# An expert's up products in 512 columns, and its transposes in one run

## The chip, the core and the metric

The kernel runs on one NeuronCore of a Trainium2 chip. The metric is the device time of one execution in microseconds, as the median of several runs. A core has five engines with a queue each: TensorE (PE in the profile, its weight loads PEld), VectorE (DVE), ScalarE (ACT), GpSimd (POOL) and SyncE (SP). Every queue is worked in its own order, and engines wait for each other by semaphores.

## The reference

The input is 4 x 2048 tokens of 512 numbers. Each token is normalised to `xn`, and the output is the input plus two branches:

```python
xn = layernorm(x)
# branch 1: random features, then a product with the features of the weights
feats   = c * exp(xn @ (xis * proj).T - 0.5 * |xn|^2 * xis^2)
attn    = feats @ weights.T                  # weights: the same features of input_weights
# branch 2: 64 experts, of which each token takes 8; CAP = 256 slots for an expert
g = einsum('ech,ehi->eci', dispatch, gate_w) # H = 512 in, I = 256 hidden
u = einsum('ech,ehi->eci', dispatch, up_w)
expert_out = einsum('eci,eih->ech', silu(g) * u, down_w)
# weighted back to the tokens, plus one shared expert for every token
out = x + attn + moe + shared(xn)
```

Everything is in float32.

## The kernel before

A float32 operand is cut into two parts in TensorE's `float32r` format: `upper` casts it on ACT, and `rest` subtracts the cast from the original on DVE. A product is then made in three passes over the same PSUM tile: upper x upper, upper x rest, rest x upper. `products` (line 103) issues these passes over the chunks of the contraction.

The execution has three stages. In the first, from the start to about 427 us, tokens are normalised, routed and transposed in blocks of 512, and every second block is finished in `dense`. The second stage is a loop over the 64 experts (lines 931 to 959). The last one works off the blocks that were left (`ends`). Between the experts, `late_attention` (line 571) works off attention products of these blocks: `ps_fu` makes features, `ps_y` multiplies them, and both lie in the PSUM pool `ps_sm` with its two buffers.

One turn of the expert loop does this for expert i:

- It asks for weights of later experts (SP's queue) and calls `hidden(i)` (line 792): for gate and up each, and for each of two halves of the hidden width, 12 products of 256 columns (4 chunks x 3 passes). The stationary operand is a 128 x 128 piece of a weight part, and the 256 columns are a part of the expert's tokens. That makes 48 products `ps_gu`. Then `gated` makes silu(g) * u from a tanh on ACT and two operations on DVE, and `upper` and `rest` cut the result into `ehT`.
- POOL's queue gets the gather for expert i + 4.
- `turn_slots(i + 1)` (line 762) transposes the tokens of the next expert, in 8 TensorE transposes `ps_t`, and cuts them into `gT`. The first one of the first expert alone is put behind an earlier product.
- `split_gates(i + 1)` cuts the next gate and up weights: two casts `gu_h` of 128 x 1024 on ACT and two subtractions `gu_l` on DVE.
- `down(i - 1)` (line 810) makes 12 products `ps_e` of 512 columns. After each six of them ACT scales the result by the token weights into `ye` (line 823), and POOL adds it to the output by an indirect DMA. Then `split_down(i)` cuts the down weights into `d_h` and `d_l`.

The program text does not give the queues' order: a scheduler in the compiler places each engine's instructions. It keeps dependencies, and the orders that `behind(a, b)` asks for. So transposes and attention products land between the expert's products where the scheduler puts them. [...] SBUF tiles of 4 KiB a partition come from the pool `four` with 40 slots.

Of the kernel before, what the change touches and what calls it, by code (L numbers as in the profile page):

```python
# [9 lines left out]
FP = mybir.dt.float32  # L10
# [3 lines left out]
ALU = mybir.AluOpType  # L14
# [4 lines left out]
P = 128  # L19
# [3 lines left out]
E = 64  # L23
# [5 lines left out]
CAP = 256  # L29
# [5 lines left out]
KC = H // P  # L35
RC = R // P
IC = I // P
# [16 lines left out]
def rfs_attention_moe_kernel(  # L54
# [15 lines left out]
    nc = tc.nc  # L70
# [5 lines left out]
    ps_mm = ctx.enter_context(tc.tile_pool(name="ps_mm", bufs=4, space=PSUM))  # L76
# [5 lines left out]
    act = ctx.enter_context(tc.tile_pool(name="act", bufs=4))  # L82

    def kib4(shape, name, dt=FPR):
        return four.tile(shape, dt, tag="four", name=name)
# [11 lines left out]
    def upper(dst, src):  # L97
        return nc.scalar.copy(dst, src)  # L98

    def rest(dst, src, hi, on=nc.vector):  # L100
        return on.tensor_tensor(dst, src, hi.bitcast(FP), ALU.subtract)  # L101

    def products(ps, w, v, start, stop):

        n = len(w)
        for part, (a, b) in enumerate(((0, 0), (0, 1), (1, 0))):
            for c in range(n):
                last["pe"] = nc.tensor.matmul(  # L108
                    ps,
                    w[c][a],  # L110
                    v[c][b],
                    start=(start and part == 0 and c == 0),
                    stop=(stop and part == 2 and c == n - 1),
                )
        return last["pe"]

    def behind(a, b):

        tc.add_manual_dep(a.ins, b.ins.name, ORDER, reason="what a needs comes late")
# [18 lines left out]
    def parts(pair, n, cols=slice(None)):  # L138
        hi, lo = pair
        return [(hi[c][:, cols], lo[c][:, cols]) for c in range(n)]  # L140
# [24 lines left out]
    last = {}  # L165
# [98 lines left out]
    def across(n):  # L264

        q = rt.tile([P, TB], FP, tag="q", name="q", bufs=3)
        nc.sync.dma_start(q, norms[n].partition_broadcast(P))
        return q
# [228 lines left out]
    def gated(dst, g, u):  # L497

        nc.scalar.activation(dst, g, AF.Tanh, scale=0.5)
        nc.vector.scalar_tensor_tensor(dst, dst, 1.0, g, ALU.add, ALU.mult)  # L500
        nc.vector.scalar_tensor_tensor(dst, dst, 0.5, u, ALU.mult, ALU.mult)  # L501

    def feature(fT, v, nsq, rc, ps):
        f = act.tile([P, TB], FP, tag="t", name="f")
        projected(v, rc, ps)
        exponent(f, nsq, rc, ps)
        nc.scalar.activation(f, f, AF.Exp, scale=ab[:, rc : rc + 1])  # L507
        upper(fT[0][rc], f)
        last["dve"] = rest(fT[1][rc], f, fT[0][rc])

    def attended(po, fT, s, start):

        return products(po, parts(fT, RC, ts(s, P)), parts(fW, RC), start, True)
# [55 lines left out]
    def fetch_block(b):  # L569

        xT = Chunks(KC, "xT_h"), Chunks(KC, "xT_l")
        for n, part in enumerate(xT):
            for k, t in enumerate(part.t):
                nc.sync.dma_start(t.bitcast(FP), turned[b // 2, n, :, 2 * k : 2 * k + 2, :])
        return xT

    def late_attention(blocks):

        blocks = list(blocks)
        nxt = fetch_block(blocks[0]), across(blocks[0])  # L580
        yield
        for n, b in enumerate(blocks):
            xu, nsq = nxt
            fT = Chunks(RC, "fU"), Chunks(RC, "fU")
            for rc in range(RC):
                ps = ps_sm.tile([P, TB], FP, tag="sm", name="ps_fu")
                feature(fT, parts(xu, KC), nsq, rc, ps)
                yield
            if n + 1 < len(blocks):
                nxt = fetch_block(blocks[n + 1]), across(blocks[n + 1])  # L590
            for s in range(NS):
                if s % 2 == 0:
                    yb = kib4([P, 2, H], "yb", FP)
                po = ps_sm.tile([P, H], FP, tag="sm", name="ps_y")
                attended(po, fT, s, True)
                last["dve"] = nc.vector.tensor_copy(yb[:, s % 2, :], po)
                if "down" in last:
                    behind(last["dve"], last["down"])
                if s % 2:
                    r0 = (b // 2) * TB + (s // 2) * UT  # L600
                    nc.sync.dma_start(
                        attn[r0 : r0 + UT, :].rearrange("(s p) d -> p s d", p=P), yb
                    )
                yield
# [20 lines left out]
    wn = across(NB)  # L625
# [28 lines left out]
    for rc in range(RC):  # L654
        pool, tag = ((ps_sm, "sm"), (ps_tr, "tr"))[rc // 2]
# [83 lines left out]
    def load_gates(e):  # L739
        gu = [kib4([P, KC, I], "gu", FP) for _ in range(2)]  # L740
        for t, w in zip(gu, (gw, uw)):
            nc.sync.dma_start(t, w[e].rearrange("(c p) i -> p c i", p=P))
        return gu

    def load_down(e):
        d = kib4([P, IC, H], "d", FP)
        nc.sync.dma_start(d, dw[e].rearrange("(c p) h -> p c h", p=P))
        return d

    def gather(e):  # L750
        xgs[e] = rows.tile([P, NH, XW], FP, tag="xw", name="xg")
        for h in range(NH):
            in_turn(
                nc.gpsimd.indirect_dma_start(  # L754
                    out=xgs[e][:, h, :],
                    out_offset=None,
                    in_=xnw,
                    in_offset=bass.IndirectOffsetOnAxis(ap=who[:, e, h : h + 1], axis=0),
                )
            )  # L760

    def turn_slots(e):
        xg = xgs.pop(e)
        xr = xg.bitcast(FPR)
        gp = [kib4([P, KC, CAP], "gT") for _ in range(2)]
        for c2 in range(KC // 2):
            pr = ps_tr.tile([P, 2, CAP], FPR, tag="tr", name="ps_t")
            ps = pr.bitcast(FP)
            for c in range(2):
                for h in range(NH):  # L770
                    turned_s = nc.tensor.transpose(  # L771
                        pr[:, c, ts(h, P)], xr[:, h, ts(c2 * 2 + c, P)], ident_r
                    )
                    if e == 0:
                        behind(turned_s, last["pe"])
            cs = slice(2 * c2, 2 * c2 + 2)
            upper(gp[0][:, cs, :], ps)
            turned_r = rest(gp[1][:, cs, :], ps, gp[0][:, cs, :])

        we = rt.tile([P, NH], FP, tag="we", name="we", bufs=4)  # L780
        shares = nc.vector.scalar_tensor_tensor(
            we, xg[:, :, H + e], 1.0, xg[:, :, H + E], ALU.add, ALU.mult
        )
        behind(shares, turned_r)
        nc.vector.reciprocal(we, we)
        wes[e] = we
        if e == 0:

            last["dve"] = shares
        return gp  # L790

    def hidden(e, gp, w):
        hi, lo = w
        v = [(gp[0][:, c, :], gp[1][:, c, :]) for c in range(KC)]
        gu = []
        for n in range(2):
            ps = ps_mm.tile([P, IC, CAP], FP, tag="mm", name="ps_gu")
            for ic in range(IC):
                wn = [(hi[n][:, c, ts(ic, P)], lo[n][:, c, ts(ic, P)]) for c in range(KC)]
                products(ps[:, ic, :], wn, v, True, True)  # L800
            gu.append(ps)
        g, u = gu
        sg = act.tile([P, IC, CAP], FP, tag="t", name="sg")
        gated(sg, g, u)
        hp = kib4([P, 2, IC, CAP], "ehT")
        upper(hp[:, 0], sg)
        last["dve"] = rest(hp[:, 1], sg, hp[:, 0])
        return hp
# [27 lines left out]
    xgs, wes, gps, gates, downs, gws, dws, hps = ({} for _ in range(8))  # L836
# [94 lines left out]
    for i in range(E + 1):  # L931


        if i + 2 < E:
            gates[i + 2] = load_gates(i + 2)
        if i + 1 < E:
            downs[i + 1] = load_down(i + 1)
        if i < E:
            hps[i] = hidden(i, gps.pop(i), gws.pop(i))
        next(slots, None)  # L940
        if i + 4 < E:
            gather(i + 4)
        if i + 1 < E:
            gps[i + 1] = turn_slots(i + 1)
            gws[i + 1] = split_gates(gates.pop(i + 1))
        for _ in range(rest_steps * i // E, rest_steps * (i + 1) // E):
            next(rest_of, None)
        if i >= E - 2:
            next(last_of)
        if i == E:  # L950

            next(last_of)
        if i > 0:
            down(i - 1, hps.pop(i - 1), dws.pop(i - 1))
        if i < E:
            dws[i] = split_down(downs.pop(i))
            if i == E - 2:

                last["down"] = last["split"]
# [40 lines left out]
```

## Time and profile before

| what | value |
|---|---|
| median of 3 runs | 1310.99 us (1310.63 to 1311.27) |
| the profiled execution | 1310.94 us, with a span of 1309.2 us |
| PE busy in the span | 1296.7 us, 99% |
| DVE busy | 925.0 us, 71% |
| ACT busy | 645.2 us, 49% |
| POOL busy | 581.7 us, 44% |
| products and transposes on PE | 7648 |

The span runs from the first instruction to the last. The 1.7 us between it and the execution's time lie outside of it. Matmuls are pipelined, so the end of a product in the profile is modelled: the pace of PE is read from the starts of rows, not from their lengths. ACT and DVE rows that follow without a wait overlap too, so what one costs its queue is also read from start to start.

### The profile page before, as it was taken

The numbers are of one execution on the slowest core, as the hardware profiler recorded it, in microseconds if no ns is written. First come the engines' busy times: TensorE is split into PE (matmuls) and PEld (weight loads), VectorE is DVE, ScalarE is ACT, GpSimd is POOL, SyncE is SP. The second block draws the span as 40 slices with busy tenths as digits, with TensorE's granted clock in tenths as the row PEclk, the third lists the DMA queues.
The fourth block names the chain that finished last, engine by engine and source line by source line (L and its number), as shares of the span: only waits on it lengthen the run. The fifth ranks groups of instructions, "written<-read, shape, count | busy, mean of one in ns | idle before, by whom it ended". The sixth has DMA issues, their size and how long they took to land.

```text
span 1309.2 us, 21368 instructions
## 1 busy us (share of the span) xinstructions
PE 1296.7 (99%) x7648; PEld 1138.6 (87%) x7648; DVE 925.0 (71%) x1922; ACT 645.2 (49%) x1017; POOL 581.7 (44%) x692
## 2 busy tenths in 40 slices
PE   8999999999999999999999999999999999999998
PEld 6888888888888999999999999999999999988886
DVE  7978768867865776777767677776776676643555
ACT  5643544354432555656566556555665566540111
POOL 3122022123106767877666667767676654210000
PEclk9999999999999999999999999999999999999999
DMA  7665675675586989999999999999999999784995
GB/s 255 242 213 205 244 279 199 238 286 212 201 307 193 317 226 330 259 290 272 304 282 266 292 272 274 246 321 262 282 256 303 280 261 233 206 239 168 318 319 193
DMA packets 189498, 338.61 MB, mean 259 GB/s; under 512 B 15952, under 2 KB 87632, under 8 KB 189392
## 3 DMA queue, kind: packets, MB, share of 16 engines
q1 hardware_dynamic: 153456, 245.93, 54.6%
q0 software_dynamic: 35936, 91.32, 29.7%
q8 instruction: 60, 0.98, 0.3%
q14 instruction: 46, 0.38, 0.1%
HBM read 220.66 MB, written 104.99 MB: 249 GB/s over the span
## 4 chain that ended last, share of the span: by engine, by line
PE 91%; DVE 4%; DMA 2%; SPq 1%; ACT 1%; issue 1%; POOL 0%; DVEq 0%; ACTq 0%
PE ps_gu L108 41%; PE ps_e L108 13%; PE ps_o L108 13%; PE ps_y L108 6%; PE ps_fu L108 6%; PE ps_f L108 4%; PE ps_t L771 3%; PE ps_x L331 2%; PE ps_l L364 2%; DMA xb<-in_L_attn_x_dram 1%; DVE st L275 1%; DMA xT_l<-turned 1%; SPq L262 1%; DVE xT_l L101 1%; DMA gu<-in_L_ffn_up_w_dram 0%
## 5 line engine op out<-in xcount | busy, mean ns | idle before, releaser
L824 POOL DMA_INDIRECT out_dram<-ye,who x128 | 225.3, 1760 | 189.3 <-ACT ye L823 140.9
L108 PE MATMUL ps_gu<-gT,gu_h 128*128 128x256 f32 x2048 | 290.0, 283 | 0.0
L108 PEld LDWEIGHTS ps_gu<-gT,gu_h 128*128 128x128 f32 x2048 | 267.2, 191 | 5.6 <-ACT gu_h L98 1.0
L701 POOL DMA_INDIRECT at<-upto,line x128 | 138.0, 1078 | 76.0 <-DVE first_of L695 37.3
L108 PE MATMUL ps_gu<-gT,gu_l 128*128 128x256 f32 x1024 | 167.0, 285 | 0.0
L101 DVE TENSOR_TENSOR gu_l<-gu,gu_h 128x1024 fp32r<-128x1024 f32 x128 | 155.7, 1218 | 6.9 <-ACT gu_h L98 6.9
L754 POOL DMA_INDIRECT xg<-xnw,who x128 | 137.3, 1073 | 39.0 <-issue 32.0
L108 PE MATMUL ps_e<-d_h,ehT 128*128 128x512 f32 x512 | 148.5, 391 | 0.0
L108 PEld LDWEIGHTS ps_gu<-gT,gu_l 128*128 128x128 f32 x1024 | 140.7, 191 | 0.3
L98 ACT CAST gu_h<-gu 128x1024 fp32r<-128x1024 f32 x128 | 132.4, 1058 | 0.0
L98 ACT CAST ehT<-sg 128x512 fp32r<-128x512 f32 x64 | 39.7, 621 | 156.3 <-DVE sg L501 156.3
L823 ACT ACTIVATE ye<-ps_e,we 128x512 f32<-128x512 f32 x128 | 88.6, 694 | 57.0 <-PE ps_e L108 56.1
L108 PEld LDWEIGHTS ps_e<-d_h,ehT 128*128 128x128 f32 x512 | 94.7, 188 | 18.8
L246 POOL TENSOR_TENSOR a<-rstd,ve 128x4 f32<-128x4 f32 x45 | 10.5, 233 | 200.1 <-DVE rstd L242 197.6
L501 DVE SCALAR_TENSOR_TENSOR sg<-sg,ps_gu 128x512 f32<-128x512 f32 x64 | 43.9, 686 | 68.4 <-PE ps_gu L108 68.0
L507 ACT ACTIVATE f<-f,ab 128x512 f32<-128x512 f32 x64 | 46.3, 723 | 82.0 <-DVE f L493 81.3
L101 DVE TENSOR_TENSOR d_l<-d,d_h 128x1024 fp32r<-128x1024 f32 x64 | 78.2, 1222 | 7.8 <-ACT d_h L98 7.4
L101 DVE TENSOR_TENSOR gT<-ps_t,gT 128x512 fp32r<-128x512 f32 x128 | 83.2, 682 | 0.2 <-ACT gT L98 0.2
L101 DVE TENSOR_TENSOR ehT<-sg,ehT 128x512 fp32r<-128x512 f32 x64 | 44.3, 692 | 51.5 <-ACT ehT L98 51.5
L108 PE MATMUL ps_o<-fW_h,fT 128*128 128x512 f32 x288 | 80.0, 392 | 0.2 <-ACT fT L98 0.2
L108 PE MATMUL ps_e<-d_l,ehT 128*128 128x512 f32 x256 | 79.3, 391 | 0.0
L108 PE MATMUL ps_o<-d_h,hT 128*128 128x512 f32 x256 | 79.1, 396 | 0.0
(181 smaller groups left out, 2526.8 us busy)
## 6 DMA issues: line engine op xcount, KB each, us to landing
gu<-in_L_ffn_gate_w_dram SPq DMA_DIRECT2D x64, 512.0 KB
gu<-in_L_ffn_up_w_dram SPq DMA_DIRECT2D x64, 512.0 KB
d<-in_L_ffn_down_w_dram SPq DMA_DIRECT2D x64, 512.0 KB
xnw<-xw SPq DMA_DIRECT2D x32, 577.0 KB
xb<-in_L_attn_x_dram SPq DMA_DIRECT2D x32, 512.0 KB
out_dram<-xb SPq DMA_DIRECT2D x32, 512.0 KB
xT_h<-turned SPq DMA_DIRECT2D x30, 512.0 KB
xT_l<-turned SPq DMA_DIRECT2D x30, 512.0 KB
```

Source lines behind the costliest of these rows:

```text
L98: return nc.scalar.copy(dst, src)
L101: return on.tensor_tensor(dst, src, hi.bitcast(FP), ALU.subtract)
L108: last["pe"] = nc.tensor.matmul(ps, w[c][a], v[c][b], start=(start and part == 0 and c == 0), stop=(stop and part == 2 and c == n - 1),)
L331: last["turn"] = nc.tensor.transpose(pr[:, ts(s, P)], src(s)[:, ts(kc, P)], ident if dt is FP else ident_r)
L364: logits = nc.tensor.matmul(pl, rwp[:, kc].rearrange("p t e -> p (t e)"), v[kc], start=(n == 0 and kc == 0), stop=(n == 1 and kc == KC - 1),)
L501: nc.vector.scalar_tensor_tensor(dst, dst, 0.5, u, ALU.mult, ALU.mult)
L507: nc.scalar.activation(f, f, AF.Exp, scale=ab[:, rc : rc + 1])
L701: nc.gpsimd.indirect_dma_start(out=at[:, e % TE, h, :], out_offset=None, in_=upto, in_offset=bass.IndirectOffsetOnAxis(ap=line[:, e, h : h ...
L754: nc.gpsimd.indirect_dma_start(out=xgs[e][:, h, :], out_offset=None, in_=xnw, in_offset=bass.IndirectOffsetOnAxis(ap=who[:, e, h : h + 1], ...
L771: turned_s = nc.tensor.transpose(pr[:, c, ts(h, P)], xr[:, h, ts(c2 * 2 + c, P)], ident_r)
L823: nc.scalar.activation(ye[:, h, :], po, AF.Copy, scale=wes[e][:, h : h + 1])
L824: now = nc.gpsimd.indirect_dma_start(out=out, out_offset=bass.IndirectOffsetOnAxis(ap=who[:, e, h : h + 1], axis=0), in_=ye[:, h, :], in_o ...
```

## The change

There are four edits.

1. In `hidden`, the gate is made as before. For up, the two token parts of a chunk lie side by side, so an upper weight part meets both of them in one product of 512 columns, and a rest weight part meets the upper token part in one of 256 columns. The left half of the PSUM tile collects two of the three passes and the right half the third. An ACT copy of the right half and a DVE addition of the left half (128 x 256 each) make `u` in SBUF. There are two such tiles for an expert, one for each half of the hidden width.
2. `turn_slots` lays `gT` out by pairs of chunks with both token parts together.
3. `turn_slots(e + 1)` is called inside `hidden(e)`, between gate and up. The first transpose of every expert is put behind the last gate product, and the next product behind the last transpose (`last["run"]`), so the eight stand together.
4. The attention results `yb` are copied from PSUM by ACT, not by DVE, and the order that kept the last ones behind a weight split is gone.

```diff
                     stop=(stop and part == 2 and c == n - 1),
                 )
+                if "run" in last:
+                    behind(last["pe"], last.pop("run"))
         return last["pe"]
...
                 attended(po, fT, s, True)
-                last["dve"] = nc.vector.tensor_copy(yb[:, s % 2, :], po)
-                if "down" in last:
-                    behind(last["dve"], last["down"])
+                nc.scalar.copy(yb[:, s % 2, :], po)
...
-        gp = [kib4([P, KC, CAP], "gT") for _ in range(2)]
+        gp = [kib4([P, 2, 2, CAP], "gT") for _ in range(KC // 2)]
...
-                    if e == 0:
+                    if c2 == c == h == 0:
                         behind(turned_s, last["pe"])
-            cs = slice(2 * c2, 2 * c2 + 2)
-            upper(gp[0][:, cs, :], ps)
-            turned_r = rest(gp[1][:, cs, :], ps, gp[0][:, cs, :])
+            upper(gp[c2][:, :, 0, :], ps)
+            turned_r = rest(gp[c2][:, :, 1, :], ps, gp[c2][:, :, 0, :])
+        last["run"] = turned_s
...
         hi, lo = w
-        v = [(gp[0][:, c, :], gp[1][:, c, :]) for c in range(KC)]
-        gu = []
-        for n in range(2):
-            ps = ps_mm.tile([P, IC, CAP], FP, tag="mm", name="ps_gu")
-            for ic in range(IC):
-                wn = [(hi[n][:, c, ts(ic, P)], lo[n][:, c, ts(ic, P)]) for c in range(KC)]
-                products(ps[:, ic, :], wn, v, True, True)
-            gu.append(ps)
-        g, u = gu
+        v = [gp[c // 2][:, c % 2] for c in range(KC)]
+        g = ps_mm.tile([P, IC, CAP], FP, tag="mm", name="ps_gu")
+        for ic in range(IC):
+            wn = [(hi[0][:, c, ts(ic, P)], lo[0][:, c, ts(ic, P)]) for c in range(KC)]
+            products(g[:, ic, :], wn, [(x[:, 0], x[:, 1]) for x in v], True, True)
+        if e + 1 < E:
+            gps[e + 1] = turn_slots(e + 1)
+        u = act.tile([P, IC, CAP], FP, tag="t", name="u")
+        for ic in range(IC):
+            ps = ps_mm.tile([P, 2, CAP], FP, tag="mm", name="ps_u2")
+            for c in range(KC):
+                for x, y in ((hi, slice(0, 2)), (lo, 0)):
+                    last["pe"] = nc.tensor.matmul(
+                        ps[:, y],
+                        x[1][:, c, ts(ic, P)],
+                        v[c][:, y],
+                        start=c == 0 and x is hi,
+                        stop=c == KC - 1 and x is lo,
+                    )
+                    if "run" in last:
+                        behind(last["pe"], last.pop("run"))
+            nc.scalar.copy(u[:, ic, :], ps[:, 1])
+            nc.vector.tensor_tensor(u[:, ic, :], ps[:, 0], u[:, ic, :], ALU.add)
         sg = act.tile([P, IC, CAP], FP, tag="t", name="sg")
         gated(sg, g, u)
...
         if i + 1 < E:
-            gps[i + 1] = turn_slots(i + 1)
             gws[i + 1] = split_gates(gates.pop(i + 1))
```

## The prediction

> **What bounds the kernel now.** I read the page first: who is full, whether TensorE runs at its full clock, and what the chain that ended last is made of.
>
> ```profile
> PE 1296.7 (99%) x7648; PEld 1138.6 (87%) x7648; DVE 925.0 (71%) x1922; ACT 645.2 (49%) x1017; POOL 581.7 (44%) x692
> PEclk9999999999999999999999999999999999999999
> PE 91%; DVE 4%; DMA 2%; SPq 1%; ACT 1%; issue 1%; POOL 0%; DVEq 0%; ACTq 0%
> ```
>
> PE is full, at full clock, and carries 91% of the chain. The sums by stage say the same of the expert stage: from 430 to 1143 us PE is busy 713.0 of 713 us, DVE 515.0, ACT 423.6, at a granted clock of 1.00. A busy PE need not be at its peak, so the next view is its timeline in a middle expert (columns: start, length, engine, line, what, count).
>
> ```profile
> 629.22 1.12 PE L108 MATMUL ps_gu<-gT,gu_h 128*128 128x256 f32 x8
> 630.18 0.64 PE L108 MATMUL ps_gu<-gT,gu_l 128*128 128x256 f32 x4
> 630.66 1.12 PE L108 MATMUL ps_gu<-gT,gu_h 128*128 128x256 f32 x8
> ...
> 632.10 0.80 PE L771 MATMUL ps_t<-ident_r,xg 128*128 128x128 f32 x8
> 632.74 1.16 PE L108 MATMUL ps_y<-fW_h,fU 128*128 128x512 f32 x4
> 633.74 1.08 PE L108 MATMUL ps_y<-fW_l,fU 128*128 128x512 f32 x4
> ...
> 636.47 1.07 PE L108 MATMUL ps_e<-d_h,ehT 128*128 128x512 f32 x4
> ...
> 638.28 1.12 PE L108 MATMUL ps_gu<-gT,gu_h 128*128 128x256 f32 x8
> ```
>
> Read from start to start: 12 products of 256 columns take 630.66 - 629.22 = 1.44 us, 0.120 each. From 633.74 to 638.28 there are 20 products of 512 columns: 4.54 us, 0.227 each. The eight transposes cost 0.64 us, and the four products behind them 1.00 instead of 0.91, so a run of eight costs 0.73. An expert's turn is 48 x 0.120 + 0.73 + 12 x 0.227 (down) + about 12 x 0.227 of attention = 11.9 us, just what the trace shows (626.35 to 638.28). There is no gap to win back, and none to spare: any late operand of PE is paid in full.
>
> Note the order at the end: attention, then down, then at once the next gate. Is the gate's weight there? ACT's timeline tells:
>
> ```profile
> 633.16 0.62 ACT L98 CAST ehT<-sg 128x512 fp32r<-128x512 f32 x1 [2.21 <-DVE sg L501]
> 633.68 1.07 ACT L98 CAST gT<-ps_t 128x512 fp32r<-128x512 f32 x2
> 634.64 1.06 ACT L98 CAST gu_h<-gu 128x1024 fp32r<-128x1024 f32 x1
> 637.12 0.69 ACT L823 ACTIVATE ye<-ps_e,we 128x512 f32<-128x512 f32 x1 [1.42 <-PE ps_e L108]
> 637.71 1.04 ACT L98 CAST gu_h<-gu 128x1024 fp32r<-128x1024 f32 x1
> 638.65 0.68 ACT L823 ACTIVATE ye<-ps_e,we 128x512 f32<-128x512 f32 x1
> ```
>
> The gate's cast `gu_h` ended at 635.70, 2.58 us before PE asked for it, because it stands ahead of both scalings `ye`. ACT's prices from these starts: `ehT` 0.52, `ye` 0.59, a cast 1.06 to its end. The sixth down product starts at 636.47 + 0.23 = 636.70 and has issued by 636.92; `ye` starts at 637.12, so PE hands over 0.20 later. From ACT to DVE or PE it is 0.03 (rows that waited). The prices of the rest are in the groups by form:
>
> ```profile
> L101 DVE TENSOR_TENSOR gu_l<-gu,gu_h 128x1024 fp32r<-128x1024 f32 x128 | 155.7, 1218 | 6.9 <-ACT gu_h L98 6.9
> L389 DVE TENSOR_TENSOR lt<-ps_lt,lt 128x256 f32<-128x256 f32 x16 | 6.7, 418 | 0.2
> L388 ACT COPY lt<-ps_lt 128x256 f32<-128x256 f32 x16 | 5.9, 368 | 12.6 <-PE ps_lt L381 10.4 <-DMA xnw<-xw 2.1
> ```
>
> **The change part by part.** *Wide products.* Per expert 24 up products of 256 become 8 of 512 and 8 of 256: 2.88 us become 8 x (0.227 + 0.120) = 2.78, -0.104; for 64 experts -6.7 us. The Trainium skill, TensorE: Matmul & The Clock Gate, section Back-to-back issue gap, gives N/2.4 + 2.5 ns, that is 109 and 216 ns. By that a merged product saves 2.5 ns and the kernel 512 x 2.5 = 1.3 us. The trace has 13 ns more than the columns need at both widths (120 - 107, 227 - 213), which gives the 6.7; I take the trace.
>
> *Transposes in one run.* Before, they stand in pieces for about half of the experts; a split of 4 + 4 costs 0.74 to 0.78 against 0.73, a split into shorter ones up to 0.1 more. -2 us (0 to -3).
>
> *DVE and ACT work.* 128 additions at 0.418 come to DVE (+53.5 us) and 28 `yb` copies at 0.686 go (-19.2): 515 + 34 of 713, no bound. ACT gets 128 copies at 0.368 and 28 at about 0.59: 424 + 64 of 713, no bound. Between up and silu's last step they add 0.2 + 0.37 + 0.42 = 1 us, hidden by the turn that lies between `hidden(i)` and `down(i)`. As busy time this is free. As places in a queue it is not.
>
> *The order of the queues.* In the built programs POOL's order is unchanged. SP has the same transfers, shifted a few places among each other; their data are asked for two experts ahead. PE and ACT are rearranged. A frequent turn:
>
> ```
>         PE                                          ACT, before the gate of the next expert
> before  gate+up 48, T 8, attention 12, down 12,     ehT, gT, gT, gu_h(gate), ye, gu_h(up), ye
> after   gate 24, T 8, up 16, down 12, attention n,  ... u, ye, ye, ehT, gu_h(gate), gu_h(up)
> ```
>
> Down now comes first and attention after it, and the scalings stand ahead of the gate's cast. ACT works in order, so the cast waits for the end of down. Counted from down's last issue to the first gate product: 0.20 hand-over + 0.59 second `ye` + 0.52 `ehT` + 1.06 cast + 0.03 = 2.40 us. PE covers it with n attention products of 0.227. Where an exponential (0.62) stands between, that is added. Then `gu_l`: it ends 0.03 + 1.22 after the cast, 8 gate products take 0.96, so another 0.29 unless two attention products stand there. The 63 turns, counted in the built order:
>
> - Both `ye` ahead of the cast, n = 0 to 2: 13 turns. Nine with n = 0 at 2.40, one with n = 2 at 1.95, three with n = 2 and an exponential at 2.57: 31.3, and 13 x 0.29 = 3.8.
> - n = 4 or 5: 6 turns, 4 x 1.50 + 2 x 1.89 = 9.8, and 1.7.
> - n = 7: 4 turns at 0.82 = 3.3, and 1.2.
> - n of 10 and more: 20 turns, most covered: 1.6 and 1.2.
> - The cast ahead of at least one `ye`: 20 turns, one of them late because `gT` stands there: 1.9 and 0.3.
>
> Sum 47.9 + 8.2 = +56 us. Beside it stand turns where another row in ACT's or DVE's queue (`u`, `fU`, `gT`) holds a cast or its subtraction: 0 to 63 x 0.29 = 18 us, +6 taken, as most have a gap to catch up in. `yb` copies now queue in ACT, and `ps_sm` has two buffers: 28 copies, each up to one cast (1.06) late, of which PE mostly finds other work; 0 to 10, +2 taken. At the end of the stage the last experts have no attention left to stand before their down: 0 to 2.7 us (12 x 0.227), +2 taken.
>
> Sum: -6.7 - 2 + 56 + 6 + 2 + 2 = +57. The profiled execution took 1310.94 (span 1309.2 and 1.7 around it), equal to the median 1310.99 to 0.05. **1368 us.** Below, an engine that catches up during the waits cannot help, since each wait starts anew from down's last product; only if ACT's handing over were twice as quick (40 us instead of 66) would it be 1342. Above, the side terms at their upper ends (18, 10, 2.7) give 1390.
>
> **The rivals.**
>
> *1. Faster.* The waits do not come, and the widths decide: 1310.94 - 8.7 = 1302. For it speaks the present trace, in which PE waits for nothing in this stage, and that ACT is idle 40% of it. Against it speaks that idle time does not move a cast ahead of a scaling in an ordered queue. It decides where the mean wait is below 8.7/63 = 0.14 us a turn, that is if the cast were mostly through before down ends. 6%.
>
> *2. Half of the waits.* Some turns hide what I count, for instance because down itself comes later on PE than I think and the queue in ACT is empty by then: half of 66 is 33, so 1335. 10%. The start of each count at down's last product speaks against it.
>
> *3. The clock falls as well.* The trace has a granted clock of 1.00 through the whole stage, and no wait in it, so it cannot show what waits of 2.4 to 2.9 us do. The Trainium skill, TensorE: Matmul & The Clock Gate, Part 1, says an idle window of about 3.4 us halves the clock. By the rule the waits are just too short; were it tripped, the next 3.4 us would do half their work, 1.7 us for each of some 20 long waits: +34, so 1402. I take the clock as full. 8%.
>
> *4. Forecast,* waits for the gate's cast: 1345 to 1390. 76%.
>
> **How the numbers follow.** 1368 is the forecast case. The range 1340 to 1395 holds that case with its bounds and the upper part of the half-wait case; it leaves out rivals 1 and 3 and part of 2. A change under about 0.2% (2.6 us) can't be told from none. Faster 0.06 is rival 1; same 0.02 needs waits that just cancel 8.7; slower 0.92 is all else.
>
> **What would show it.** Right: PE is no longer full in the expert stage (about 90%), PE or PEld rows of `ps_gu` get idle time "<-ACT gu_h" of 2.4 us in about nine turns, and some 8 us "<-DVE gu_l"; the chain shows ACT `ehT`, `ye` and `gu_h`, several per cent where 1% was. The 512-wide up products stand 0.227 apart and the 256-wide 0.120, and a run of transposes costs 0.73. Wrong: PE stays at 99%; or the idle time before `ps_gu` is under 20 us in all; or it is put down to a DMA of weights or `gT`; or the granted clock drops in the stage.

## The result, and the profile after

The changed kernel takes 1386.87 us (median of 5, 1386.07 to 1390.67) against 1311.27 before (median of 5): ratio 1.0585, 95% interval 1.0573 to 1.0596, slower. The profiled execution took 1386.57 us with a span of 1384.8, so the two spans differ by 75.6 us. All of it lies in the expert stage: the first expert's first gate product starts at 426.9 us (before 427.1), the last expert's last up product at 1217.7 (before, the last of the 48 products: 1141.9), and what comes behind takes 167.1 us (before 167.3).

The page of the changed kernel, the three lines that answer to those shown in the prediction:

```profile
PE 1320.4 (95%) x7136; PEld 1121.5 (81%) x7136; DVE 958.4 (69%) x2022; ACT 696.5 (50%) x1173; POOL 598.4 (43%) x692
PEclk9999999999999999999999999999999999999999
PE 78%; DVE 9%; ACT 4%; DMA 4%; issue 3%; POOL 1%; SPq 1%; DVEq 0%; ACTq 0%; POOLq 0%
```

PE does 512 products fewer, and is no longer full: in the expert stage it is busy for 738.6 of 788 us. On the chain it falls from 91% to 78%; DVE and ACT together rise from 5% to 13%. The waits of the weight loads (columns: total, times, longest) say for what:

```profile
PEld ps_gu L108 <- ACT gu_h L98: 57.2, 39, 2.7
PEld ps_gu L108 <- DVE gu_l L101: 12.0, 28, 1.1
```

One turn of the changed kernel's timeline, with no attention product between down and the next gate:

```profile
731.38 0.61 PE L108 MATMUL ps_e<-d_h,ehT 128*128 128x512 f32 x2
...
732.03 0.69 ACT L842 ACTIVATE ye<-ps_e,we 128x512 f32<-128x512 f32 x1 [0.68 <-PE ps_e L108]
732.61 0.61 ACT L98 CAST ehT<-sg 128x512 fp32r<-128x512 f32 x1
733.12 2.00 ACT L98 CAST gu_h<-gu 128x1024 fp32r<-128x1024 f32 x2
...
734.20 2.36 DVE L101 TENSOR_TENSOR gu_l<-gu,gu_h 128x1024 fp32r<-128x1024 f32 x2 [0.25 <-ACT gu_h L98]
734.22 1.00 PEld L108 LDWEIGHTS ps_gu<-gT,gu_h 128*128 128x128 f32 x8 [2.65 <-ACT gu_h L98]
...
735.48 0.53 PEld L108 LDWEIGHTS ps_gu<-gT,gu_l 128*128 128x128 f32 x4 [0.26 <-DVE gu_l L101]
```

This is the chain of the prediction, link by link. Down's last product starts at 731.38 + 0.23 = 731.61 and has issued by 731.84; the second scaling starts 0.19 later, `ehT` 0.58 behind it, the cast 0.51 behind that, and the gate's first product at 734.22. From 731.84 that is 2.38 us; the prediction had 2.40. Eight products later PE stands again until `gu_l` is made.

What the forecast left out is in the sums by short windows. The clock row of the page is too coarse for it: each digit stands for 35 us. In windows of 3.41 us (columns: window, length, PE, PEld, DVE, ACT, POOL busy, granted clock, DMA):

```profile
730.44:733.85 3.41, 1.55 (x7) 0.94 (x5) 1.96 (x6) 2.51 (x4) 1.92 (x2) 1.00 0.91 339
744.10:747.51 3.41, 1.16 (x8) 0.80 (x7) 1.69 (x3) 3.41 (x5) 2.80 (x3) 1.00 1.05 311
747.51:750.92 3.41, 3.41 (x18) 3.31 (x16) 3.41 (x5) 1.57 (x3) 2.80 (x3) 0.50 0.80 111
750.92:754.33 3.41, 3.41 (x26) 3.11 (x26) 0.88 (x2) 0.75 (x2) 1.79 (x2) 1.00 0.64 133
```

PE's rows in the second and third of these windows:

```profile
746.72 1.45 PE L108 MATMUL ps_gu<-gT,gu_h 128*128 128x256 f32 x8 [2.25 <-ACT gu_h L98]
...
749.00 1.91 PE L108 MATMUL ps_gu<-gT,gu_h 128*128 128x256 f32 x8
750.71 0.50 PE L108 MATMUL ps_gu<-gT,gu_l 128*128 128x256 f32 x2
```

In the window from 744.10 PE waits 2.4 us for `gu_h` (2.25 by the modelled end of the product before). In the next one it has all it needs, but the granted clock is 0.50: eight products of 256 columns take 750.71 - 749.00 = 1.71 us from start to start, 0.214 each where 0.120 is usual. There are ten such windows in the expert stage, each 3.41 us long; before there was none in the stage.

### The profile page after: what moved, and what is told of

It reads as the page before. It is cut to its first block, busy times and chain, and to the rows that moved or that the text cites. A ratio compares the mean times of both kernels' runs of the same rounds, so it can differ in the third digit from the quotient of the medians.

```text
span 1384.8 us, 20432 instructions
## 1 busy us (share of the span) xinstructions
PE 1320.4 (95%) x7136; PEld 1121.5 (81%) x7136; DVE 958.4 (69%) x2022; ACT 696.5 (50%) x1173; POOL 598.4 (43%) x692
## 4 chain that ended last, share of the span: by engine, by line
PE 78%; DVE 9%; ACT 4%; DMA 4%; issue 3%; POOL 1%; SPq 1%; DVEq 0%; ACTq 0%; POOLq 0%
PE ps_gu L108 25%; PE ps_u L811 12%; PE ps_o L108 12%; PE ps_e L108 11%; PE ps_fu L108 4%; PE ps_y L108 4%; PE ps_f L108 3%; PE ps_t L772 3%; DVE gu_l L101 2%; PE ps_l L366 2%; PE ps_x L333 1%; ACT gu_h L98 1%; DMA xb<-in_L_attn_x_dram 1%; ACT ehT L98 1%; DVE st L277 1%
## 5 line engine op out<-in xcount | busy, mean ns | idle before, releaser
L108 PE MATMUL ps_gu<-gT,gu_h 128*128 128x256 f32 x1024 | 156.5, 298 | 42.0 <-ACT gu_h L98 41.8
L108 PEld LDWEIGHTS ps_gu<-gT,gu_h 128*128 128x128 f32 x1024 | 141.6, 202 | 59.8 <-ACT gu_h L98 57.2
L811 PE MATMUL ps_u<-gT,gu_h 128*128 128x512 f32 x512 | 185.9, 403 | 0.0
L811 PE MATMUL ps_u<-gT,gu_l 128*128 128x256 f32 x512 | 143.1, 279 | 0.0
L821 DVE TENSOR_TENSOR u<-ps_u,u 128x256 f32<-128x256 f32 x128 | 54.0, 422 | 122.8 <-ACT u L820 122.8
L811 PEld LDWEIGHTS ps_u<-gT,gu_h 128*128 128x128 f32 x512 | 95.9, 187 | 19.4
L108 PE MATMUL ps_gu<-gT,gu_l 128*128 128x256 f32 x512 | 91.4, 304 | 6.2 <-DVE gu_l L101 5.2
L811 PEld LDWEIGHTS ps_u<-gT,gu_l 128*128 128x128 f32 x512 | 96.6, 189 | 0.0
L108 PEld LDWEIGHTS ps_gu<-gT,gu_l 128*128 128x128 f32 x512 | 77.1, 205 | 14.6 <-DVE gu_l L101 12.0
L98 ACT CAST gT<-ps_t 128x512 fp32r<-128x512 f32 x128 | 69.1, 598 | 28.1 <-PE ps_t L772 28.1
```

Source lines behind the costliest of these rows:

```text
L108: last["pe"] = nc.tensor.matmul(ps, w[c][a], v[c][b], start=(start and part == 0 and c == 0), stop=(stop and part == 2 and c == n - 1),)
L811: last["pe"] = nc.tensor.matmul(ps[:, y], x[1][:, c, ts(ic, P)], v[c][:, y], start=c == 0 and x is hi, stop=c == KC - 1 and x is lo,)
L821: nc.vector.tensor_tensor(u[:, ic, :], ps[:, 0], u[:, ic, :], ALU.add)
```

## The experiments

Two theories were to be told apart, beside smaller ones. Theory 1: the place of the gate's cast in ACT's order makes the waits, and long waits make the half-clock windows. Theory 2: the added work itself, 128 copies, 128 additions and one more PSUM tile for each expert (five, from the four buffers of the pool `ps_mm`), costs the time.

**Move one call (e1, and again e9).** The changed kernel with the split ahead of silu. Nothing of the new work is taken away.

```diff
+        if e + 1 < E:
+            gws[e + 1] = split_gates(gates.pop(e + 1))
         sg = act.tile([P, IC, CAP], FP, tag="t", name="sg")
...
-        if i + 1 < E:
-            gws[i + 1] = split_gates(gates.pop(i + 1))
```

> The changed kernel with one call moved: split_gates(i + 1) inside hidden(i), between the up products and gated(), so that the casts gu_h stand ahead of ehT and both ye in ACT's order. All products, additions and copies stay. Theory 1 (the place of the gate's cast in ACT's order makes the waits, and the waits make the half-clock windows): PE's waits for gu_h and gu_l in the expert stage fall from about 54 us to under 5, no half-clock window is left in the stage, and the wide products' 6.7 us and the transposes' 2 us come out: 1302 to 1307 us, faster than before. Theory 2 (the added work itself costs: 128 copies, 128 additions, a fifth PSUM tile per expert): the time stays above 1360.

Measured: 1318.66 us against 1326.95 for the kernel before on that chip, ratio 0.9922 (0.9895 to 0.9948). Both times lie above what was expected. In the four kernels profiled on that chip (e1 to e4) the expert stage begins only at 434 to 448 us, where it is 427 in the two main traces. Late transfers are the likely reason, but the traces do not name them. So the run is read by its expert stage: 708.4 us, against 714.9 in the trace of before and 790.8 in that of the changed kernel. The time was taken again on a chip where the kernel before takes its usual time:

> The kernel of the moved split once more, to have its time beside a kernel before that takes 1311 us: in the first comparison both waited for transfers ahead of the expert stage, which has nothing to do with the change. From the stage's length there, 708.4 us against 714.9, it should take 1303 to 1306 us, a ratio of 0.994 to 0.997. If the moved split helped only with those late transfers, the ratio is 1.00 here.

Measured: 1302.32 us against 1310.78, ratio 0.9935 (0.9921 to 0.9948), slightly below the expected range. Its page and ACT's timeline:

```profile
PE 1287.4 (99%) x7136; PEld 1108.7 (85%) x7136; DVE 957.0 (74%) x2022; ACT 696.3 (54%) x1173; POOL 604.4 (46%) x692
PE 85%; DVE 5%; DMA 4%; SPq 2%; POOL 1%; issue 1%; ACT 1%; POOLq 0%; ACTq 0%; DVEq 0%
```

```profile
731.75 1.05 ACT L98 CAST gu_h<-gu 128x1024 fp32r<-128x1024 f32 x1
...
733.13 1.05 ACT L98 CAST gu_h<-gu 128x1024 fp32r<-128x1024 f32 x1
734.08 0.60 ACT L501 ACTIVATE sg<-ps_gu 128x512 f32<-128x512 f32 x1
736.99 0.69 ACT L844 ACTIVATE ye<-ps_e,we 128x512 f32<-128x512 f32 x1 [2.30 <-PE ps_e L108]
737.57 0.61 ACT L98 CAST ehT<-sg 128x512 fp32r<-128x512 f32 x1
738.35 0.69 ACT L844 ACTIVATE ye<-ps_e,we 128x512 f32<-128x512 f32 x1 [0.16 <-PE ps_e L108]
```

And the first gate product of the same turn on PE:

```profile
737.69 0.62 PE L108 MATMUL ps_e<-d_h,ehT 128*128 128x512 f32 x2
738.15 1.12 PE L108 MATMUL ps_gu<-gT,gu_h 128*128 128x256 f32 x8
```

The gate's cast ends at 732.80, 5.35 us before PE asks for it at 738.15, and the gate follows down without a gap (0.46 us for down's last two products). ACT is as busy as in the changed kernel (696.3 and 696.5 us) and DVE too (957.0 and 958.4), yet the span is 83.4 us shorter. The waits of weight loads for `gu_h` in the stage are 1.3 us, and the clock is 1.00.

The moved call also let the scheduler rearrange PE, so one may ask whether that helped instead. In PE's trace 50 of the 62 turns now have no attention product between down and the next gate, against 9 in the changed kernel, so PE has less to cover a late cast with. But the cast is no longer late: in the median turn it ends 2.9 us before the first gate product, and in the changed kernel 0.05 us before it. Theory 2 falls, and theory 1 carries the whole slowdown. This version is faster than the kernel before by 0.65%.

**The same place of the split in the kernel before (e3).** It could have been a gain of its own.

```diff
         g, u = gu
+        if e + 1 < E:
+            gws[e + 1] = split_gates(gates.pop(e + 1))
         sg = act.tile([P, IC, CAP], FP, tag="t", name="sg")
...
             gps[i + 1] = turn_slots(i + 1)
-            gws[i + 1] = split_gates(gates.pop(i + 1))
```

> The kernel before with only split_gates(i + 1) moved into hidden(i), ahead of gated(). A control for the moved split: if the place of the casts is worth nothing where they were already in time (theory 1), it is within 3 us of 1311. If the earlier place is a gain of its own, it is 5 us or more faster, and the moved split's gain would not be the wide products'.

Measured: 1328.96 us against 1326.95 on that chip, ratio 1.0009 (0.9994 to 1.0023). The place is worth nothing where the cast was in time already. The stage of this run is 725.0 us long, but the excess lies in its first 40 us, with the late start of that chip: from the fifth expert's first gate product to the last up product it takes 674.5 us, and 672.6 in the trace of before. So the gain of e9, 8.5 us, does not come from the moved call; it belongs to the changed kernel's own edits.

**The tie of the transposes (e2, e10).** The moved split without `last["run"]`, and with only the first expert's transposes placed by hand.

> The kernel of the moved split, with the eight transposes no longer tied together (only the first expert's are placed by hand; the call stays between gate and up). Theory 1: as with the moved split, no waits to speak of, 1302 to 1308. It tells what tying the transposes is worth: by the trace of before a split 4 + 4 costs 0.01 to 0.05 us more than a run of eight, so at most 2 us slower than the moved split. If the tie were what costs, this one would be faster by over 5 us.

> The moved split without the tied transposes once more, beside the tied one on the same chip. The trace of the changed kernel puts the tie at about 2 us (63 switches between transposes and products instead of about 110, at 0.08 each, less somewhat dearer transposes): 1305 to 1308, or within 1 us of the tied one if the tie is worth nothing.

Measured: e2 has a ratio of 0.9931 (0.9904 to 0.9959) to the kernel before, and e1 on the same chip 0.9922. e10 takes 1304.52 us (1302.63 to 1305.47) beside e9's 1302.32 (1301.94 to 1303.43), just under its expected range. The medians differ by 2.2 us, but the runs overlap. The traces are steadier. From the fifth expert's first gate product to the last up product the tied versions take 664.5 (e1) and 664.9 us (e9), the untied ones 666.0 (e2) and 665.8 (e10). So the tie is worth some 1.0 to 1.5 us there. The untied versions have 83 switches from transposes to products against 63, and 110 in the kernel before.

**Edit 3 alone (e4).** Narrow products, transposes between gate and up in one run.

```diff
             gu.append(ps)
+            if n == 0 and e + 1 < E:
+                gps[e + 1] = turn_slots(e + 1)
...
-            gps[i + 1] = turn_slots(i + 1)
```

The lines that tie the run, `last["run"]` and the two `behind`, are as in the change.

> The kernel before with edit 3 alone: transposes of the next expert between gate and up, tied into one run; gate and up products stay narrow, yb stays on DVE. In its built order attention still stands ahead of down and the cast ahead of the scalings for most turns, so theory 1 has no waits to expect: 1308 to 1312 (the run saves 2 us, the rest 0). Theory 3 (the transposes' new place makes ACT late, whatever the products): over 1340.

Measured: ratio 1.0006 (0.9986 to 1.0027), an expert stage of 713.8 us against 714.9. The transposes' place makes ACT hardly late: weight loads wait for `gu_h` 12 times, 4.0 us in all, where it was 1.0 before. The 2 us that the run should save do not show in the time; in the stage it is 1.1.

**Edits 1, 2 and 4 without edit 3 (e5).** The transposes' call is back behind `hidden`, and they are not tied.

> Edits 1, 2 and 4 without edit 3: wide up products, but the transposes called where they were before and not tied. Laid out with the durations of before, its built order has about 5 us of waits of gate products for gu_l and about 9 us of waits of transposes for a PSUM tile of ps_tr, no wait over 1.5 us, so no half-clock window: -6.7 + 14 + some waits on yb = 1316 to 1326. If edit 1 alone made the waits for gu_h, it would be over 1350; if it made none at all, 1304.

Measured: 1335.47 us, ratio 1.0190 (1.0173 to 1.0207). This was above what I expected, by 9 us and more. The waits of its weight loads:

```profile
PEld ps_t L772 <- DVE gT L101: 21.0, 43, 1.7
PEld ps_gu L108 <- ACT gu_h L98: 5.3, 23, 0.5
```

Here the gate's cast is nearly in time. It is the transposes that wait, for DVE to read their PSUM tile; the pool `ps_tr` holds two. Part of the 21 us of their weight loads runs beside products: by the starts of PE's rows the transposes lose 11.5 us, near the 9 laid out. The rest of the miss lies in 158 switches from transposes to products instead of 110 (about 4 us more, not laid out), in gate products that lose 8.5 us to all their operands (5 laid out), and in attention products that lose 3.1. So neither part of the change alone makes waits for `gu_h` of more than about 5 us; they come with the order that the scheduler gives to both together. Why it chose that order was not tried.

**The cast ahead of the scalings only (e6).** Both `ye` are put behind the gate's cast, which stays behind `ehT`.

```diff
...
-            nc.scalar.activation(ye[:, h, :], po, AF.Copy, scale=...)
+            scaled = nc.scalar.activation(ye[:, h, :], po, AF.Copy, scale=...)
+            if e + 2 < E:
+                behind(scaled, last["gate"])
```

The lines left out keep the gate's cast as `last["gate"]` when `split_gates` makes it.

> The changed kernel with one order more: both ye of a turn behind the gate's cast. The cast still stands behind ehT, which waits for silu's last step: from up's end 0.20 + 0.37 copy + 0.42 addition + 0.69 last step + 0.52 ehT + 1.06 cast and three hand-overs of 0.03, less 2.72 of down, is about 0.6 at best, and 1.6 where u's copy stands behind gT. Theory 1: waits of at most 1.9 us, sum 30 to 42 instead of 54, and windows with little idle time, so at most two half-clock windows instead of ten: 1338 to 1352. If the half-clock windows come from the new mix of products and not from long waits, about ten stay and it is over 1358.

```profile
PEld ps_gu L108 <- ACT gu_h L98: 33.9, 30, 1.9
PEld ps_gu L108 <- DVE gu_l L101: 10.8, 27, 1.1
```

Measured: 1350.05 us, ratio 1.0300 (1.0282 to 1.0317), with one half-clock window in the stage. The longest wait fell from 2.7 to 1.9 us and the sum of the two lines from 69.2 to 44.7, and nine of ten half-clock windows went with it, though the products are those of the changed kernel (in places in another order). The clock follows the waits, not the mix of products.

**The disputed cost doubled (e7).** The up weights' cast ahead of the gate's.

```diff
-        return list(zip(*(split(t, "gu") for t in gu)))
+        up = split(gu[1], "gu")
+        return list(zip(split(gu[0], "gu"), up))
```

> The changed kernel with the two splits of a turn exchanged: the up weights' cast first, then the gate's. It doubles the disputed cost: the gate's cast ends one cast (0.95 us) later. Theory 1: the waits of gate products grow by 25 to 40 us, waits of 3 us and more fill whole windows, and the half-clock windows rise from 10 to 20 or more: 1425 to 1450. If the wait is for something else in the turn (the scaling's DMA, gT, a PSUM tile), the exchange does nothing: within 5 us of 1387.

```profile
PEld ps_gu L108 <- ACT gu_h L98: 89.4, 45, 3.6
PEld ps_gu L108 <- DVE gu_l L101: 21.2, 37, 1.8
PEld ps_y L108 <- ACT fU L98: 15.9, 6, 3.1
```

Measured: 1462.61 us, ratio 1.1157 (1.1139 to 1.1176), with 26 stretches at half clock in the stage, 24 of them of one window and two of two. Exchanging two casts of the same size costs 75.7 us more than the changed kernel, which had run on another chip (the kernel before takes 1310.54 us on this one and 1311.27 on that one). I had 1450 at most: the waits grew by 32 + 9 us, as laid out, but 16 us of waits of attention products for their own cast `fU`, now late as well, were not in it.

**Edit 4 undone (e8).** `yb` is copied by DVE again.

> The changed kernel with edit 4 undone: attention results are copied by DVE again, with the old order at the end. By the prediction yb on ACT was worth 2 us of waits of ps_y: 1382 to 1388, and the waits for gu_h stay within 5 us. If the copies in ACT's queue are what makes the casts late, it falls by 10 us or more.

Measured: 1385.69 us in a single run, with ten half-clock windows. ACT's copies of `yb` are not the cause.

## Why the prediction was right, point by point

The number was forecast at 1368 with a range of 1340 to 1395; it was 1386.87. To see which terms carried it, I took the starts of PE's products in the expert stage of both profiled executions and set 0.120 us (256 columns), 0.227 (512) and 0.078 (a transpose) off each interval. What is left is a wait, a switch from transposes to products, or a half-clock window. The split covers the whole difference, so that it adds up proves nothing; and the first row is a count of products at these paces.

| term | forecast, us | measured, us |
|---|---|---|
| wide products | -6.7 | -6.7 |
| transposes in one run | -2 | -2.3 |
| gate products waiting for `gu_h` and `gu_l` | 56 + 6 | 64.6 |
| attention products waiting for `yb` | 2 | 2.8 |
| down at the end of the stage | 2 | 2.5 |
| half-clock windows | 0 | 14.7 |
| sum | 57 | 75.6 |

- *PE has no slack, so a late operand is paid in full.* Right: the spans differ by 1384.8 - 1309.2 = 75.6, and its largest term, 64.6, is gate products that wait for their weights.
- *Wide products, 13 ns saved per product merged.* Right. An upper part and a rest part take 0.347 us together in the changed kernel (the median of 449 pairs), where three narrow products take 0.360; and e9, without the waits, is 8.5 us faster than before, where 8.7 were forecast for the wide products and the transposes together. By the formula in the Trainium skill, TensorE: Matmul & The Clock Gate, section Back-to-back issue gap, which is meant there for an isolated product, it would be 1.3 us: far too low here.
- *Busy time of ACT and DVE is free.* Right: e9 keeps all of it and is faster than before.
- *The order of the queues.* Right, and the core of it. The hand sum over the 63 turns was 62 with its side term and is measured at 64.6. It holds turn by turn too: nine turns without attention products wait 2.39 us for the gate's cast (forecast 2.40), one with two of them 1.94 (1.95), four with four of them 1.48 (1.50), four with seven 0.81 (0.82). Only the three with an exponential wait less, 2.42 or 2.43 for 2.57. All waits at the first gate product come to 47.3 us, forecast 47.9. Rival 1 (1302 us, if the cast were through before down ends) is what e9 brought about on purpose: 1302.32.
- *The clock taken as full* is the step that failed. The prediction held the waits "just too short" for a rule of a whole idle window. The runs show that a window needs only some 60% of idle time: ten windows at half clock, 14.7 us, about 1.5 us each. This was rival 3, with 34 us for twenty windows; half as many came. Without the term the sum is 61 and the time 1372. A clock that drops in the stage was also among the prediction's own signs of being wrong. That the time still fell into the range is in part luck: the room above 1368 had been left for the side terms, which needed little of it. With twenty windows at these 1.5 us it would have been about 1401.

## What to carry to other kernels

An engine at half load can still stop a full one: read in which order the queue stands, and count from the last thing that its head waits for to the operand that the full engine needs next. When a change rearranges a scheduler's order, first move the late producer ahead in the program text, and judge the change by that version: here one moved call made 1.0585 into 0.9935. Look at the clock in short windows, too: here a wait of about 2.4 us that fell into one of them cost about 1.5 us more at half clock. So long waits are worth shortening first, as e6 did; cutting one in two was not tried.

## What the runs showed of the hardware

The granted clock changes on a fixed grid of 3.41 us: all half-clock windows of the stage start a multiple of that apart. Idle time of PE is counted here from a product's start plus its pace to the next start. In the changed kernel every window with 2.17 us or more of it is followed by one at half clock, and none with 1.87 or less is; of three with 2.02 to 2.05 us one is. In e6, e7 and e8 the border lies between 1.9 and 2.1 as well. So a wait's place on the grid counts as well as its length. The 2.4 us in the window from 744.10 halved the next one. The equally long wait in the turn shown above, which began at 731.84 and ended at 734.22, lies across the border at 733.85, left 2.03 us of idle time in its window, just at the border, and cost nothing more. After a half-clock window in which PE is busy the clock is full again (the window from 750.92). In the two stretches of e7 that lasted two windows, PE was busy for only 2.34 and 2.64 us of the first, and the clock stayed at half. The Trainium skill, TensorE: Matmul & The Clock Gate, Part 1, has the window's length and that it runs free; its idle window of 3.4 us as the condition is more than these traces need.

ACT's instructions that follow without a wait start about 0.10 us before the one ahead ends (two casts of 1.05 in 2.00 us above), DVE's about 0.08 (two subtractions of 1.22 in 2.36 us). A sum made with the groups' mean lengths (0.69 + 0.62 + 1.06, and the hand-overs 0.20 and twice 0.03) would have had the long wait at 2.63 us instead of 2.40; 2.38 was measured.
